# Program order for layer 2's scalings, and ScalarE for layer 3's transpose copies

## The chip, the cores and the metric

The kernel runs on one core of one Trainium2 chip. The metric is the device time of one execution, in microseconds (us). A core has five engines that run side by side and meet at semaphores: TensorE for matmuls and transposes (PE in the profile, PEld for its weight loads), VectorE (DVE), ScalarE (ACT), GpSimd (POOL) and SyncE (SP), which only issues transfers. Transfers are issued from the queues of SP, ACT and POOL.

## What is computed

The program is a chain of four residual layers on 8 images of 56 x 56 pixels with 192 channels. Each layer first normalises its input over 32 groups of channels, then adds what it computes to it:

```python
x = x + toeplitz_gated_unit(_gn(x))      # layer 0
x = x + window_attention(_gn(x))         # layer 1
x = x + L2(_gn(x))                       # layer 2
x = x + L3(_gn(x))                       # layer 3

def L2(x):
    proj = x @ W_in + b_in                       # 192 -> 384 channels
    local = depthwise_conv_3x3(proj)
    mixed = 0.25 * (lr + rl + tb + bt) + local   # decaying sums in four directions
    return layernorm(mixed) @ W_out + b_out

def L3(x):
    y = layernorm(depthwise_conv_7x7(x))
    return (gelu(y @ w0 + b0) @ w1 + b1) * gamma
```

The change touches the entry of layer 2 (its group normalisation, and the transfer of its first image) and the entry of layer 3 (the copies behind its transposes). All data is float32.

## The kernel before

The image is held with channels on the partitions, its upper half in partitions 0 to 63 and its lower half in 64 to 127, as three chunks of 64 channels. Stages follow one another, each a loop over the 8 images; between some of them the data goes through DRAM, since the convolutions run over all images with channels as the outer loop.

**Layer 2's projection** (about 3570 to 3860 us). `layer2_image` (line 787) makes a tile `x2` from a pool of two, clears its border rows on GpSimd and loads two halves on the queue that it is given. The loop at line 1313 starts the load of image b+1 on SP and then calls `layer2_in` for image b. That function (line 797) makes `xn`, the normalised image: three scalings on VectorE, one for each chunk (line 803), and two edge memsets on GpSimd (lines 806 and 807). Then come 15 groups of matmuls into four PSUM buffers (line 815), each followed by a bias add on VectorE (line 823) that writes the projected tile `pt`, and the store of `pt` to DRAM on SP. `xn` and `pt` have two buffers each. At line 1310 the first image is loaded on POOL's queue; the two lines after it load the weights on ACT's queue. After the sixth image, line 1318 finishes the last image's group statistics. Ahead of the stage, layer 1's last image is stored by rows: 54 stores on SP at line 612, of which 30 fall after 3553 us.

No order is written by hand in this stage. A scheduler places the instructions of each engine by its own estimate of when their inputs are ready; it may put an instruction of a later image ahead of one of an earlier image if it takes the former for ready sooner.

**The joint stage** (about 4521 to 5040 us) makes layer 2's output and layer 3's input together. It runs in 8 x 4 groups of rows: for each group three output channels chunks j are multiplied (`layer2_out`, line 960) and added to the image (line 965), while the next group is scaled (lines 936 on VectorE and 938 on ScalarE), transposed (line 947) and evacuated from PSUM on ScalarE (line 948). In the steps 3 to 8 of an image's twelve, VectorE also takes the layer norm statistics of the next image (line 190). Between these go the steps of the generator `layer3_in` (line 968) for the image before: its group statistics, three normalising scalings on GpSimd (line 985), and then, for each of three chunks, 15 transposes in four PSUM tiles (line 1006) with the copies into `zt` (lines 993 and 995), and a store of `zt` to DRAM. From two PSUM buffers the first and third tile are copied by VectorE, the second and fourth by ScalarE; the fourth has two extra single-row copies, one on each engine. VectorE's order in this stage is the program's own (`manual_schedule`), that of TensorE and ScalarE is the scheduler's. The last image's `layer3_in` runs alone at the end of the stage.

Of the kernel before, what the change touches and what calls it, by code (L numbers as in the profile page):

```python
# [52 lines left out]
PH = NPAIR // 2  # L53
# [24 lines left out]
def kernel(ctx: ExitStack, tc: tile.TileContext, a: dict, out: bass.AP):  # L78
    nc = tc.nc
# [61 lines left out]
    def gn_piece(st, x, t):  # L141

        for j in range(3):
            nc.vector.bn_stats(st[:, j, t], x[:, j, bass.ts(t, TT)])

    def gn_aggregate(st, mv):
        for j in range(3):
            nc.vector.bn_aggr(mv[:, j, :], st[:, j].rearrange("p t s -> p (t s)"))

    def gn_finish(mv, sc, sh, pool, psum, ptag):  # L150


        n = mv.shape[1]

        def over_groups(v, name):
            if ptag == "mm":
                ps = psum.tile([128, 512], F32, name=name, tag="mm", bufs=3)
            elif ptag == "y":
                ps = psum.tile([128, TT], F32, name=name, tag="y")
            elif ptag == "gn":  # L160
                ps = psum.tile([128, 3], F32, name=name, tag="gn", bufs=1)
            else:
                ps = psum.tile([128, 2, 512], F32, name=name, tag=ptag)[:, 0]
            ps = ps[:, 0:3 * n].rearrange("p (n j) -> p n j", j=3)
            for j in range(3):
                ks = [k for k in range(3) if abs(j - k) < 2]
                for k in ks:
                    nc.tensor.matmul(
                        ps[:, :, j], gmath[:, 2 * k + j, :], v[:, :, k], start=(k == ks[0]), stop=(k == ks[-1])
                    )  # L170
            return ps

        mean = pool.tile([128, n, 3], F32, name="gh_mean")
        nc.vector.tensor_copy(mean, over_groups(mv[:, :, :, 0], "gh_m"))
        d = pool.tile([128, n, 3], F32, name="gh_d")
        nc.vector.tensor_tensor(d, mv[:, :, :, 0], mean, ALU.subtract)
        nc.vector.tensor_tensor(d, d, d, ALU.mult)
        nc.vector.tensor_tensor(d, d, mv[:, :, :, 1], ALU.add)
        yield
        nc.scalar.activation(sc, over_groups(d, "gh_v"), AF.Sqrt, bias=eps5)  # L180
        nc.vector.reciprocal(sc, sc)
        nc.vector.scalar_tensor_tensor(sh, mean, -1.0, sc, ALU.mult, ALU.mult)

    def run(steps):
        for _ in steps:
            pass
# [152 lines left out]
    def layer0_load(b, pool):  # L339
        x = pool.tile([128, 3, NH], F32, name="x0")  # L340
        nc.gpsimd.dma_start(x, a["x"][b])
        return x
# [444 lines left out]
    def layer2_image(b, xpool, queue):  # L787

        x = xpool.tile([128, 3, R2, W], F32, name="x2")
        nc.gpsimd.memset(x[0:64, :, 0], 0.0)  # L790
        nc.gpsimd.memset(x[64:128, :, R2 - 3:R2], 0.0)
        src = x2[b].rearrange("(j p) (h w) -> p j h w", p=64, w=W)
        queue.dma_start(x[0:64, :, 1:R2], src[:, :, 0:R2 - 1])
        queue.dma_start(x[64:128, :, 0:R2 - 3], src[:, :, R2 - 1:H])
        return x

    def layer2_in(b, x, pool, psum, w_in, b_in):

        sc, sh = scsh2[:, b, 0], scsh2[:, b, 1]
        xn = pool.tile([128, 3, R2, 64], F32, name="xn2")  # L800
        nc.gpsimd.memset(xn[:, :, :, W:64], 0.0)
        for j in range(3):
            nc.vector.tensor_scalar(
                xn[:, j, :, 0:W], x[:, j], sc[:, j:j + 1], sh[:, j:j + 1], ALU.mult, ALU.add
            )
        nc.gpsimd.memset(xn[0:64, :, 0, 0:W], 0.0)
        nc.gpsimd.memset(xn[64:128, :, R2 - 3:R2, 0:W], 0.0)
        pt = pool.tile([128, C2, P2], F32, name="pt")
        nh = R2 // 2
        for i in range(nh):  # L810
            ns = 2 if i + nh < P2 else 1
            ps = psum.tile([128, 2, 512], F32, name="pin")
            for j in range(3):
                for s in range(ns):
                    nc.tensor.matmul(
                        ps[:, s, 0:C2], xn[64 * s:64 * s + 64, j, 2 * i:2 * i + 2].rearrange("p h w -> p (h w)"),
                        w_in[64 * s:64 * s + 64, j], start=(j == 0), stop=(j == 2),
                    )

            v = 0 if i == 0 else 2 if i + nh == P2 - 1 else 1  # L820
            dims = [list(z) for z in pt.ap]
            dst = bass.AP(pt.tensor, pt.offset + i, [dims[0], [nh, ns], [P2, C2]])
            nc.vector.tensor_tensor(dst, ps[:, 0:ns, 0:C2], b_in[:, v, 0:ns], ALU.add)

        n = CG2 if b + 1 == nimg else 0
        if n:
            nc.sync.dma_start(pd[b][:, 0:n], pt[:, 0:n])
        nc.sync.dma_start(pd[b][:, n:C2], pt[:, n:C2])
# [139 lines left out]
    def layer3_in(b, x, zp, pool, psum):  # L968

        sc = pool.tile([128, 1, 3], F32, name="sc3")  # L970
        sh = pool.tile([128, 1, 3], F32, name="sh3")
        st = pool.tile([128, 3, NTH, 6], F32, name="gh_st")
        mv = pool.tile([128, 1, 3, 2], F32, name="gh_mv")
        for t in range(NTH):
            gn_piece(st, x, t)
            if t % 2:
                yield
        gn_aggregate(st, mv[:, 0])
        finish = gn_finish(mv, sc, sh, pool, psum, "gn")
        next(finish)  # L980
        yield
        run(finish)

        for j in range(3):
            nc.gpsimd.tensor_scalar(
                zp[:, j, 1:H // 2 + 1, 0:W], x[:, j].rearrange("p (h w) -> p h w", w=W),
                sc[:, 0, j:j + 1], sh[:, 0, j:j + 1], ALU.mult, ALU.add,
            )
        yield

        def to(dst, src, eng):
            if eng:
                nc.scalar.copy(dst, src)
            else:
                nc.vector.tensor_copy(dst, src)

        for j in range(3):
            zt = pool.tile([OP, 64, NB], F32, name="zt")
            nc.gpsimd.memset(zt[:, :, 0:1], 0.0)
            nc.gpsimd.memset(zt[:, :, NB - 1:NB], 0.0)  # L1000
            for g, m0 in enumerate(range(0, PH + 1, 4)):
                yield
                tp = psum.tile([OP, 4, 2, 64], F32, name="zps")
                nm = min(4, PH + 1 - m0)
                for i in range(nm):
                    nc.tensor.transpose(  # L1006
                        tp[:, i].rearrange("p s c -> p (s c)"),
                        zp[:, j, 2 * (m0 + i):2 * (m0 + i) + 2].rearrange("p h w -> p (h w)"), ident,
                    )

                n2 = min(nm, PH - m0)
                dst = zt[:, :, 1 + m0:1 + m0 + n2]
                dst = bass.AP(dst.tensor, dst.offset, [list(dst.ap[0]), [1, n2], [PH, 2], [NB, 64]])
                to(dst, tp[:, 0:n2], g % 2)
                if nm > n2:

                    to(zt[:, :, 1 + 2 * PH], tp[:, n2, 1], 0)
                    to(zt[0:64, :, 1 + PH], tp[0:64, n2, 0], 1)
            nc.sync.dma_start(zd[b][:, 64 * j:64 * j + 64], zt)

    def convolve(first, dwb):
# [50 lines left out]
    def layer3_image(b, pool):  # L1072
        x = pool.tile([128, 3, NH], F32, name="x3")
        nc.sync.dma_start(x, xd[b])
        return x
# [100 lines left out]
    with ExitStack() as st:  # L1176
# [6 lines left out]
        x = layer0_load(0, pool)  # L1183
# [8 lines left out]
        for b in range(nimg):  # L1192
# [12 lines left out]
            if b + 1 < nimg:  # L1205
                x = layer0_load(b + 1, pool)
# [5 lines left out]
    with ExitStack() as st:  # L1212
# [8 lines left out]
        images, x = ExitStack(), []  # L1221
# [13 lines left out]
    with ExitStack() as st:  # L1235
# [20 lines left out]
        xpool = x.pop(0)  # L1256
# [49 lines left out]
    with ExitStack() as st:  # L1306
        xpool = st.enter_context(tc.tile_pool(reuse_waits="tile", name="l2x", bufs=2, side="right"))
        pool = st.enter_context(tc.tile_pool(reuse_waits="tile", name="l2i", bufs=2))
        psum = st.enter_context(tc.tile_pool(reuse_waits="tile", name="l2ip", bufs=4, space=PSUM))
        x = [layer2_image(0, xpool, nc.gpsimd)]  # L1310
        w_in = resident("w_in", nc.scalar, pool)
        b_in = resident("b_in", nc.scalar, pool)
        for b in range(nimg):
            if b + 1 < nimg:
                x.append(layer2_image(b + 1, xpool, nc.sync))
            layer2_in(b, x[b], pool, psum, w_in, b_in)
            if b == nimg - 3:
                run(gn_finish(mv2[:, last], scsh2[:, last, 0], scsh2[:, last, 1], pool, psum, "pin"))
    with ExitStack() as st:
# [8 lines left out]
        x = [load_halves(pool, x2[0], "x2o")]  # L1328
# [54 lines left out]
    with ExitStack() as st:  # L1383
# [9 lines left out]
        x = [layer3_image(0, pool)]  # L1393
# [122 lines left out]
```

## Time and profile before

| what | us |
|---|---|
| median of 3 runs (6226.7 to 6247.08) | 6227.99 |
| the profiled execution | 6250.54 |
| its span, first to last instruction | 6248.8 |
| TensorE, busy | 5549.3 (89%) |
| VectorE, busy | 3450.3 (55%) |
| ScalarE, busy | 2251.5 (36%) |
| GpSimd, busy | 1328.0 (21%) |
| line 803, scalings (24) | 26.1 busy, 1145 ns each |
| line 815, matmuls (1392) | 237.7 busy, 47.6 idle ahead |
| line 823, bias adds of 768 elements (112) | 169.9 busy, 1542 ns each |
| line 995, copies of 512 (48) and of 64 elements (24) on VectorE | 51.7 and 6.6 busy, 1077 and 276 ns each |
| line 993, copies of 512, 256 and 64 elements (24 each) on ScalarE | 26.1, 15.0 and 6.5 busy, 1089, 627 and 269 ns each |

Busy time is the time in which an engine has an instruction of its own running. Idle time ahead is the time an engine stood still before the instructions of a group; it counts only where that engine sets the pace. In the lines of the profile an arrow in square brackets names what ended the wait.

### The profile page before, as it was taken

Reading aid. Unit: us, or ns where it says so; the run is one execution under the profiler, and the core shown is the slowest. Engines: PE = TensorE matmul, PEld = TensorE weight load, DVE = VectorE, ACT = ScalarE, POOL = GpSimd, SP = SyncE. Lnnn points to the kernel's source line nnn. Section 1 sums busy time; section 2 is a strip of 40 time slices with the busy share of each in tenths; the row PEclk is TensorE's granted clock in tenths of the full one; section 3 lists DMA queues with packets and bytes.
Section 4 is the critical chain, followed back from the end, with each engine's and each line's share of the span. In section 5 each row is a group of like instructions: output and inputs, shape, how many; then the busy total and the mean of one; then the engine's idle time right before and its main releaser. Section 6 shows DMA issues by size and latency. Waiting matters only on the chain. (4 is left out here: it accounts for less than half of the span.)

```text
span 6248.8 us, 126609 instructions
## 1 busy us (share of the span) xinstructions
PE 5549.3 (89%) x55636; PEld 3585.7 (57%) x55636; DVE 3450.3 (55%) x4800; ACT 2251.5 (36%) x2932; POOL 1328.0 (21%) x869
## 2 busy tenths in 40 slices
PE   6799989999999888888888688999888889799999
PEld 5577766666666454445444466767544479544444
DVE  5677766556565344444444376888788710433331
ACT  2334444344444233333333200445455510233333
POOL 1100025444444122121212101333300100110100
PEclk8899989999999888878888798999999989899999
DMA  6799986666665515545442586677667579421210
GB/s 165 186 216 214 191 242 255 264 261 258 256 256 213 80 34 60 60 60 56 56 48 41 67 239 226 209 232 239 189 167 208 162 288 331 154 82 64 72 57 24
DMA packets 1034540, 1013.11 MB, mean 162 GB/s; under 512 B 826136, under 2 KB 958196, under 8 KB 1007220
## 3 DMA queue, kind: packets, MB, share of 16 engines
q1 hardware_dynamic: 1019424, 940.93, 54.0%
q0 software_dynamic: 8832, 41.81, 2.2%
q10 hardware_dynamic: 5732, 22.27, 1.1%
q8 instruction: 437, 7.16, 0.5%
q14 instruction: 115, 0.94, 0.0%
HBM read 676.28 MB, written 345.08 MB: 163 GB/s over the span
## 5 line engine op out<-in xcount | busy, mean ns | idle before, releaser
L371 PE MATMUL qv<-w_qv_sb,xn 64*112 64x288 f32 x5376 | 722.1, 425 | 50.3 <-DVE act L377 46.9
L409 POOL COPY lc<-lt 128x896 f32<-128x896 f32 (+1 forms) x320 | 572.1, 1805 | 624.5 <-PE op L417 608.4
L371 PEld LDWEIGHTS qv<-w_qv_sb,xn 64*112 64x112 f32 x5376 | 535.0, 184 | 232.5 <-DVE act L377 63.2
L378 ACT ACTIVATE act<-act 112x576 f32<-112x576 f32 x448 | 299.9, 682 | 462.8 <-DVE act L377 425.8
L1145 PE MATMUL ph<-y,w_sb 64*128 64x392 f32 x2304 | 398.4, 498 | 6.5 <-ACT hid L1149 6.5
L429 PE MATMUL pj<-xn,w_p_sb 64*128 64x392 f32 (+1 forms) x1920 | 374.0, 516 | 14.0 <-issue 10.7
L1156 PE MATMUL po<-hid,w_sb 128*64 128x392 f32 x2304 | 386.3, 494 | 0.0
L417 PEld LDWEIGHTS op<-rc,lc 128*56 128x56 f32 x9216 | 310.6, 137 | 127.2 <-issue 61.8
L417 PE MATMUL op<-rc,lc 128*56 128x56 f32 x9216 | 342.1, 222 | 45.2 <-POOL lc L409 26.1
L450 PE MATMUL y<-pp,w_o_sb 128*64 128x392 f32 (+1 forms) x1920 | 357.3, 505 | 18.9 <-DVE x L458 10.2
L377 DVE TENSOR_TENSOR act<-qv,b_qv 112x576 f32<-112x576 f32 x448 | 320.7, 751 | 85.4 <-PE qv L371 85.0
L1163 DVE TENSOR_TENSOR x<-x,z 128x392 f32<-128x392 f32 x96 | 70.4, 733 | 522.8 <-ACT z L1161 522.8
L409 ACT COPY rc<-rt 128x896 f32<-128x896 f32 (+1 forms) x160 | 256.9, 1606 | 240.6 <-PE op L417 226.7
L727 POOL TENSOR_TENSOR e<-e,mx 128x1176 f32<-128x1176 f32 x64 | 139.9, 2185 | 954.3 <-DVE mx L726 899.4
L866 PE MATMUL cv<-zc,wt 128*128 128x224 f32 x1536 | 313.7, 356 | 24.1 <-DMA zc<-pd 24.1
L866 PEld LDWEIGHTS cv<-zc,wt 128*128 128x128 f32 x1536 | 290.9, 190 | 67.8 <-issue 51.6
L443 DVE TENSOR_TENSOR pp<-pp,ot 128x784 f32<-128x784 f32 (+1 forms) x160 | 154.6, 966 | 306.6 <-ACT pp L434 288.3
L677 PE MATMUL qk_ps<-xr,wg 64*96 64x392 f32 x1536 | 309.7, 512 | 15.1 <-ACT qk L683 13.5
L1145 PEld LDWEIGHTS ph<-y,w_sb 64*128 64x128 f32 x2304 | 220.4, 189 | 176.4 <-issue 26.0
L1046 PE MATMUL cps<-zc,wt 128*128 128x224 f32 x1536 | 299.5, 356 | 18.0 <-DMA zc<-zd 17.6
L1046 PEld LDWEIGHTS cps<-zc,wt 128*128 128x128 f32 x1536 | 289.5, 189 | 27.8 <-issue 20.4
L1156 PEld LDWEIGHTS po<-hid,w_sb 128*64 128x64 f32 x2304 | 162.6, 137 | 213.8 <-issue 213.8
(211 smaller groups left out, 9423.0 us busy)
## 6 DMA issues: line engine op xcount, KB each, us to landing
lt<-left SPq DMA_DIRECT2D x72, 1792.0 KB
rt<-right SPq DMA_DIRECT2D x72, 1792.0 KB
left<-qv SPq DMA_DIRECT2D x224, 252.0 KB
right<-qv SPq DMA_DIRECT2D x448, 126.0 KB
wt<-in_band_dram SPq DMA_DIRECT2D x23, 2048.0 KB
wt<-in_band_dram SPq DMA_DIRECT2D x11, 4096.0 KB
zc<-pd SPq DMA_DIRECT2D x187, 232.0 KB
pd<-pt SPq DMA_DIRECT2D x7, 5568.0 KB
```

Source lines behind the costliest of these rows:

```text
L371: nc.tensor.matmul(ps[s][:, which, 0:D1 // 2], xn[64 * s:64 * s + 64, j, bass.ts(i, 2 * W)], w_qv[64 * s:64 * s + 64, j, which, ns], start ...
L377: nc.vector.tensor_tensor(act, ps[s][:, :, 0:D1 // 2], b_qv[:, :, ns], ALU.add)
L378: nc.scalar.activation(act, act, AF.Silu)
L409: copy(c[:, 0:nu], raw.rearrange("p (w u d) -> p u d w", u=nu, d=64 // nu)[:, :, d0:d0 + 8])
L417: nc.tensor.matmul(op[64 * u:64 * u + W, i, :], lc[:, u, i], rc[:, u, i], start=True, stop=True)
L429: nc.tensor.matmul(ps[0:M, s, 0:TT], w_p[64 * s:64 * s + 64, j, d0:d0 + M], xn[64 * s:64 * s + 64, j, ts], start=(j == 0), stop=(j == 2),)
L450: nc.tensor.matmul(y[64 * s:64 * s + 64], w_o[0:M, c, 64 * j:64 * j + 64], pp[0:M, s], start=(c == gated[0][0]), stop=(c == gated[-1][0]),)
L677: nc.tensor.matmul(ps[s], wg[64 * s:64 * s + 64, j, c0:c0 + HC], xw[64 * s:64 * s + 64, j, gs], start=(j == 0), stop=(j == 2),)
L866: nc.tensor.matmul(dst, wt[:, c4 + i, 128 * q:128 * q + 128], zc[:, :, c4 + i, q:q + NPAIR], start=(q == 0), stop=(q == 1),)
L1046: nc.tensor.matmul(dst.rearrange("p (b n) -> p b n", n=NPAIR), wt[:, c4 + i, q * OP:(q + 1) * OP], zc[:, :, c4 + i, q:q + NPAIR], start=(q ...
L1145: nc.tensor.matmul(ps[:, s, 0:TT], w0[64 * s:64 * s + 64, j, m * 128:(m + 1) * 128], y[64 * s:64 * s + 64, j, ts], start=(j == 0), stop=(j ...
L1156: nc.tensor.matmul(ps[64 * s:64 * s + 64], w1[:, m, 64 * j:64 * j + 64], hid[:, m, s], start=(m == 0), stop=(m == 5),)
```

## The change

Three edits. The scalings of `layer2_in` are wrapped in `tc.keep_in_program_order`, which pins an instruction behind the one that was written before it on the same engine (an order alone, not a wait for its end). The copies behind layer 3's transposes all go to ScalarE. The first image of layer 2 is loaded on ACT's queue.

```diff
@@ layer2_in
         for j in range(3):
-            nc.vector.tensor_scalar(
+            tc.keep_in_program_order(nc.vector.tensor_scalar(
                 xn[:, j, :, 0:W], x[:, j], sc[:, j:j + 1], sh[:, j:j + 1], ALU.mult, ALU.add
-            )
+            ))
@@ layer3_in
-        def to(dst, src, eng):
-            if eng:
-                nc.scalar.copy(dst, src)
-            else:
-                nc.vector.tensor_copy(dst, src)
-
         for j in range(3):
...
-            for g, m0 in enumerate(range(0, PH + 1, 4)):
+            for m0 in range(0, PH + 1, 4):
...
-                to(dst, tp[:, 0:n2], g % 2)
+                nc.scalar.copy(dst, tp[:, 0:n2])
                 if nm > n2:
-                    to(zt[:, :, 1 + 2 * PH], tp[:, n2, 1], 0)
-                    to(zt[0:64, :, 1 + PH], tp[0:64, n2, 0], 1)
+                    nc.scalar.copy(zt[:, :, 1 + 2 * PH], tp[:, n2, 1])
+                    nc.scalar.copy(zt[0:64, :, 1 + PH], tp[0:64, n2, 0])
@@ layer 2's projection
-        x = [layer2_image(0, xpool, nc.gpsimd)]
+        x = [layer2_image(0, xpool, nc.scalar)]
         w_in = resident("w_in", nc.scalar, pool)
         b_in = resident("b_in", nc.scalar, pool)
```

In the program that the scheduler makes of it, VectorE's order in the projection is: the three scalings of an image, its 15 bias adds, the three scalings of the next image, and so on. On ACT's queue the first image's two loads stand behind both weight loads.

## The prediction, made before the changed kernel ran

> **What bounds the kernel now.** The chain of waits at the foot of the page is of little use: its shares add up to 22%, and asked for the stretch from 4460 us on it begins at 4937.03. So I went by stages. The line groups gave the start of each stage, a table of windows gave the busy time in it, and the timeline gave what happens at its edges. The columns of the windows are the stretch and its length, then busy time (count) of PE, PEld, DVE, ACT and POOL, the granted clock, the DMA share and GB/s.
>
> ```profile
> 3569.00:3616.00 47.00, 0.33 (x2) 0.33 (x4) 6.66 (x8) 1.28 (x1) 2.25 (x4) 0.53 0.73 140
> 3616.00:3860.00 244.00, 242.04 (x1420) 169.85 (x1418) 196.42 (x145) 0.26 (x1) 15.53 (x35) 0.97 0.68 223
> 4521.00:5040.00 519.00, 431.19 (x2395) 229.02 (x2393) 397.81 (x737) 274.03 (x389) 52.98 (x72) 0.92 0.62 180
> ```
>
> Row one is the gap ahead of layer 2's projection: 47 us with no engine at work. Row two is that projection: TensorE is busy 242.04 of 244 us, so nothing but TensorE sets its length. Row three is the joint stage (layer 2's output and layer 3's input): no engine is full over the whole of it.
>
> The timeline shows what ended the gap, and how an image follows the last:
>
> ```profile
> 3595.48 0.59 SPq L793 DMA_DIRECT2D x<-x  x1
> 3610.03 6.48 DVE L803 TENSOR_SCALAR xn<-x,scsh 128x1680 f32<-128x1680 f32 x6 [40.30 <-DMA x<-x]
> 3615.67 176.30 PE L815 MATMUL pin<-w_in_sb,xn 64*128 64x384 f32 x1044 [47.62 <-POOL xn L806]
> 3646.88 0.85 DVE L823 TENSOR_TENSOR pt<-pin,b_in_sb 128x384 f32<-128x384 f32 x1 [0.39 <-PE pin L815]
> 3647.57 3.26 DVE L803 TENSOR_SCALAR xn<-x,scsh 128x1680 f32<-128x1680 f32 x3
> 3650.89 0.23 POOL L806 MEMSET xn<- 64x168 f32 x1 [3.22 <-DVE xn L803]
> ```
>
> Six scalings stand together at 3610.03: those of images 0 and 1. In the built program image 1's first piece is ahead of image 0's three, so image 0 (loads issued at 3563.31 and 3563.97, landed 17.7 us after the second) waits for image 1, loaded at 3595.48. In exchange VectorE is one image ahead: the scalings at 3647.57 are image 2's, and TensorE runs 176.30 us without a break.
>
> For the joint stage, three windows inside one image's period, and the edge between the first two:
>
> ```profile
> 4861.00:4888.00 27.00, 19.69 (x121) 10.21 (x120) 26.79 (x45) 9.76 (x18) 0.33 (x2) 0.96 0.52 127
> 4888.00:4900.00 12.00, 10.23 (x48) 7.30 (x47) 6.56 (x12) 10.70 (x14) 0.33 (x2) 0.66 0.98 258
> 4900.00:4923.00 23.00, 22.81 (x131) 11.51 (x132) 16.14 (x37) 14.25 (x19) 1.42 (x1) 1.00 0.81 269
> ...
> 4886.33 1.17 DVE L995 COPY zt<-zps 128x512 f32<-128x512 f32 x2
> ...
> 4887.53 1.94 PE L1006 MATMUL zps<-ident,zp 128*128 128x128 f32 x8 [4.66 <-DVE zt L995]
> ```
>
> VectorE fills the first (26.79 of 27), ScalarE nearly the second (10.70 of 12), TensorE the third (22.81 of 23). The waits view says the same of the stage: layer 3's transposes wait for VectorE's copies 45.1 us (matmul) and 17.6 us (weight load), for ScalarE's 10.1 and 15.6.
>
> [...]after its 4.66 us gap the 5 us from 4887.5 have clock 0.50, and the 3.4 us behind the like gaps that end at 4698.0 and 4759.6 have 0.52 and 0.51. [...]from 3568 to 3580 the queues of POOL, ACT and SP have shares of 76.3, 22.6 and 4.7%, together one. [...]
>
> **Part 1, the scalings keep program order.** In the built program of the changed kernel each image's three scalings stand behind the last bias add of the image before. The look-ahead is gone at all seven edges between images. At each, TensorE now waits for: the last bias add (3646.88 to the next instruction, 0.69), three scalings (3.26), the step to GpSimd (0.06), its edge memset (0.23), the step back (about 0.05): 4.3 us. It waited for nothing there before. The gap is of the size that halves the clock: 3.4 to 5 us at half speed cost 1.7 to 2.5, I take 1.9. At the edge from image 5 to 6 the group statistics already stop TensorE (3791.9 to 3797.6, half clock to 3803.8), so only the 4.3 is added. Sum: 6 x (4.3 + 1.9) + 4.3 = 41.5 us. Nothing hides it, since TensorE is the bound of the stage. Bounds: 30 (no clock loss) to 50. Behind the waiting scalings stand only the next image's bias adds, which need them anyway; behind the stores on SP stand loads that have an image's time (some 33 us) to land. No cost there.
>
> **Part 2, image 0's load on ACT's queue.** It leaves POOL, where it was issued at 3563.31, and in the built order stands behind both weight loads on ACT; its two halves wait besides for one each of the last row stores of layer 1's image 7. In the old run the 30 stores left SP between 3553.68 and 3594; from 3568 to 3580 they got 4.7% because POOL's load took 76.3%. Without it they can end up to 12 us sooner, near 3583. Then image 0's and image 1's loads (2352 KB, or 2.41 MB, each) run beside one another: 4.82 MB at the 207 GB/s of 3600 to 3608 is 23.3 us, plus 2.9 to start (image 1's took 14.55 = 11.6 + 2.9): both land near 3608, image 0 some 2 to 3 us sooner, say 3605. Three scalings and a memset later TensorE starts, at 3608.6 in place of 3615.67: 7 us gained. Bounds: 16 gained (image 0 gets the engines alone) to 8 lost (the stores end as late as before).
>
> Layer 2's projection in sum: 41.5 - 7 = +34.5, between +20 and +50.
>
> **Part 3, copies in the joint stage.** VectorE loses 72 copies (51.7 + 6.6 us), ScalarE gains as many of the same length. They count where VectorE is the bound: in the window of 27 us it makes copies of 1.14, 1.23, 1.10 and 1.17 us, 4.64 in sum; 22.4 us of other work stay, above TensorE's 19.69. So the statistics, the next image's scalings and its first transposes come 4 to 4.6 us sooner[...]. Given back: in the new order ScalarE takes the copies in pairs, those of the third piece later, among layer 2's evacuations where TensorE is full; a pair (2.2 us) ahead of an evacuation holds the next transposes up by about 1 us. I take 3.7 net in each of 6 images. In the last image's period VectorE has no statistics ahead (13.67 busy of 29 between 4981 and 5010): nothing. In the tail after 5026.96 both engines copied in turn in 12.0 us; ScalarE alone needs 9 x 1.09 + 3 x 0.63 + 6 x 0.27 = 13.3 and its steps: +1.7. Sum: -22.2 + 1.7 = -20.5, between -42 and 0.
>
> **Sum.** 34.5 - 20.5 = +14. Against the profiled execution's own 6250.54 us that is 6264.5. That execution is 0.36% above the median of the runs shown, so I put the change on the median: 6228 + 14 = 6242 us. A measurement of this kernel can tell 0.3%, or 18.7 us, from no change.
>
> **Rivals.**
> - *Forecast* (0.52): both effects as above, from -8 to +32; slower by over 0.3% in 0.22 of it, within in 0.30.
> - *Not slower: the joint stage gives back more* (0.21). Place: the edge at 4887.53. If the copies (4.64), the rest of the gap and its half clock (2.5) all go, 7 us an image are saved: 6 x 7 - 1.7 = 40, and the sum is -6, or 6222 us. It decides from (34.5 + 1.7)/6 = 6.0 us an image; past 9.1, or with small clock losses, it is faster by over 0.3%. For it: 62.7 us of waits on VectorE's copies. Against: ScalarE is full in the next window. Faster 0.12, within 0.09.
> - *ScalarE becomes the joint stage's bound* (0.20): with the copies moved it has 338 of 519 us in all, and 10.70 of 12 in one window already. Nothing is gained there, the tail costs 1.7: +36, 6264 us. Slower.
> - *Image 0 arrives late* (0.07): the row stores take as long as before, and the loads share: part 2 turns to +8, sum +29, 6257 us. Slower 0.05, within 0.02.
>
> Sums: faster 0.12, within 0.3% 0.41, slower 0.47. The range takes the rivals in and leaves out a tenth at each end: 6212 to 6272.
>
> **What would show it.** Right: seven TensorE gaps of some 4.3 us ahead of the projection's matmuls, ended by GpSimd's memset, each with a dip in the clock; 275 to 290 us from the first to the last of these matmuls in place of 243; the first of them near 3608; no transposes of layer 3 waiting for VectorE; the period of an image in the joint stage near 58 us where it was 61.7. Wrong: no gaps, or scalings that run while matmuls do; a start before 3600 or after 3616; a joint stage shorter by over 40 us, or no shorter at all.

## The result, and the profile after

The changed kernel takes 6237.23 us, the median of 12 runs (6212.07 to 6248.5), and the kernel before, run beside it, 6229.72 us, also of 12 (6216.59 to 6249.95). The two medians are 7.5 us apart; over all runs the ratio is 1.0005, or +3 us, with a 95% interval from 0.9992 to 1.0019, in time between 5 us less and 12 us more. That is no difference that this measurement can tell. Behind it stand three effects of 17 to 44 us that cancel.

The profiled execution of the changed kernel has a span of 6230.6 us, 18.2 less than that of before. This says nothing of the change: layers 0 and 1, whose code is the same, ended 18.9 us sooner in it (last matmul of layer 1 at 3549.20 in place of 3568.05 us). So stages are compared here by their own lengths, and the start of the projection is counted from that last matmul. Line numbers of the changed kernel differ: the scalings are line 804, the upper edge memset 807, the projection's matmuls 816, layer 3's transposes 1001 and their copies 1009.

The windows view of the changed kernel, cut at the edges of its own stages (columns as in the prediction):

```profile
3549.20:3579.78 30.58, 0.00 (x0) 0.00 (x1) 5.14 (x8) 1.28 (x1) 2.63 (x3) 0.56 0.74 156
3579.78:3867.28 287.50, 256.36 (x1420) 148.91 (x1420) 201.22 (x146) 0.26 (x1) 14.39 (x33) 0.92 0.61 196
4522.59:5019.54 496.95, 434.55 (x2394) 224.00 (x2393) 350.33 (x665) 315.39 (x458) 53.14 (x72) 0.92 0.64 187
```

| stage | before | after | difference |
|---|---|---|---|
| last matmul of layer 1 to first of the projection | 47.62 | 30.58 | -17.0 |
| projection, first to last matmul | 243.31 | 287.50 | +44.2 |
| joint stage, first output matmul to last transpose of layer 3 | 516.50 | 496.95 | -19.5 |
| sum | | | +7.6 |

The timeline of the changed kernel at the start of the projection and at the edge from image 1 to image 2:

```profile
3561.26 0.69 ACTq L793 DMA_DIRECT2D x<-x  x1
3561.99 0.72 ACTq L794 DMA_DIRECT2D x<-x  x1
3575.87 3.57 DVE L804 TENSOR_SCALAR xn<-x,scsh 128x1680 f32<-128x1680 f32 x3 [24.99 <-DMA x<-x]
3576.10 1.09 POOL L790 MEMSET x<- 64x168 f32 x1 [31.63 <-DMA x<-x]
3576.11 0.59 SPq L793 DMA_DIRECT2D x<-x  x1
3579.78 31.27 PE L816 MATMUL pin<-w_in_sb,xn 64*128 64x384 f32 x174 [30.58 <-POOL xn L807]
...
3647.65 0.84 DVE L824 TENSOR_TENSOR pt<-pin,b_in_sb 128x384 f32<-128x384 f32 x1 [0.39 <-PE pin L816]
3648.33 3.25 DVE L804 TENSOR_SCALAR xn<-x,scsh 128x1680 f32<-128x1680 f32 x3
3651.64 0.23 POOL L807 MEMSET xn<- 64x168 f32 x1 [3.21 <-DVE xn L804]
3651.93 30.98 PE L816 MATMUL pin<-w_in_sb,xn 64*128 64x384 f32 x174 [4.32 <-POOL xn L807]
```

In its first part, image 0 waits for nothing but its own load and starts alone; the load of image 1 leaves SP at 3576.11, when that of image 0 has just landed. In the second, a bias add, three scalings and a memset stand one behind the other, and TensorE waits 4.32 us for them. Each of the seven edges looks like this, and an image that took 29.3 us from its first matmul to its last in the kernel before takes 31.0 to 32.3 us behind its gap.

For the joint stage, two groups of the kernel before and the same two of the changed kernel (busy time and mean, then the idle time ahead and what ended it):

```profile
L1006 PE MATMUL zps<-ident,zp 128*128 128x128 f32 x360 | 61.2, 308 | 57.9 <-DVE zt L995 45.1 <-ACT zt L993 10.1 <-POOL zp L985 2.6
L947 PE MATMUL tp<-ident,yt 112*128 112x112 f32 x672 | 104.0, 289 | 39.7 <-DVE yt L936 34.3 <-ACT y L948 5.3
...
L1001 PE MATMUL zps<-ident,zp 128*128 128x128 f32 x360 | 56.8, 299 | 6.5 <-ACT zt L1009 3.5 <-POOL zp L986 2.6
L948 PE MATMUL tp<-ident,yt 112*128 112x112 f32 x672 | 106.6, 290 | 66.1 <-DVE yt L937 57.7 <-ACT y L949 7.9
```

Layer 3's transposes no longer wait for VectorE (before: 45.1 us), and for ScalarE's copies only 3.5 us. In place of that, layer 2's own transposes (the second row of each pair) wait longer for VectorE's scaled rows, 57.7 us where they waited 34.3: VectorE still sets the pace at the edge inside an image, with less to do.

### The profile page after: what moved, and what is told of

It is laid out like the page before. It is cut to its first block, busy times and chain, and to the rows that moved or that the text cites. A ratio compares the mean times of both kernels' runs of the same rounds, so it can differ in the third digit from the quotient of the medians.

```text
span 6230.6 us, 126592 instructions
## 1 busy us (share of the span) xinstructions
PE 5550.5 (89%) x55636; PEld 3552.3 (57%) x55636; DVE 3403.1 (55%) x4728; ACT 2293.7 (37%) x3004; POOL 1320.7 (21%) x867
## 5 line engine op out<-in xcount | busy, mean ns | idle before, releaser
L429 PE MATMUL pj<-xn,w_p_sb 64*128 64x392 f32 (+1 forms) x1920 | 375.2, 517 | 14.5 <-issue 10.8
L816 PE MATMUL pin<-w_in_sb,xn 64*128 64x384 f32 x1392 | 253.0, 514 | 60.8 <-POOL xn L807 60.8
```

The lines of the kernel that those rows point to most:

```text
L429: nc.tensor.matmul(ps[0:M, s, 0:TT], w_p[64 * s:64 * s + 64, j, d0:d0 + M], xn[64 * s:64 * s + 64, j, ts], start=(j == 0), stop=(j == 2),)
```

## The experiments

All ratios are against the kernel before, run beside each on the same chip, with 95% intervals; the kernel before had medians of 6216 and 6215 us there, so one thousandth is 6.2 us. The stages in the traces are compared with the one trace of the kernel before. Two of the kernels below leave layer 2's start as it was (the copies alone, and VectorE's time put back): there TensorE starts 44.33 and 44.35 us behind layer 1's last matmul, and the projection takes 241.69 and 243.21 us, in place of 47.62 and 243.31. So a start is known to some 3 us, and each gain at the start that is given below may be about 3 us too large.

### The program order alone

```diff
+            tc.keep_in_program_order(nc.vector.tensor_scalar(
```

(on all scalings; the first image stays on GpSimd's queue, the copies as before)

> The kernel before with the program order alone. In the changed kernel TensorE began the projection 30.6 us after its last matmul of layer 1 (before: 47.6), and the projection then took 287.5 us (before: 243.3). Theory: the order does both. It costs the seven edges (+44), and it frees image 0 from waiting for image 1; image 0 still comes on GpSimd's queue here, where it landed 13.6 us after the last matmul, so TensorE should begin some 18 us after it, 30 us sooner than before: sum +14, near 6244, ratio 1.0022. Rival: the sooner start came from the other queue, which lets the row stores through. Then the start stays near 47 us, sum +44, near 6273, ratio 1.007.

Measured: ratio 1.0041 (1.0028 to 1.0054), or +25 us. In the trace the projection takes 287.98 us, and it starts 25.33 us behind layer 1's last matmul. The timeline of this kernel shows what the start waited for:

```profile
3540.95 3.28 DVE L803 TENSOR_SCALAR xn<-x,scsh 128x1680 f32<-128x1680 f32 x3 [10.47 <-DMA x<-x]
3553.00 0.59 SPq L793 DMA_DIRECT2D x<-x  x1
3553.00 0.23 POOL L790 MEMSET x<- 64x168 f32 x1 [27.66 <-DMA x<-x]
3553.27 0.52 POOL L791 MEMSET x<- 64x504 f32 x1
3553.84 0.23 POOL L806 MEMSET xn<- 64x168 f32 x1
3554.13 2.29 PE L815 MATMUL pin<-w_in_sb,xn 64*128 64x384 f32 x6 [25.33 <-POOL xn L806]
```

The scalings of image 0 end at 3544.25, 15.4 us behind that last matmul, as the theory had it. But the edge memset that TensorE needs stands on GpSimd behind two memsets for image 1's tile, and these wait for layer 1's row stores until 3553.00. So the order costs +44.7 and gains 22.3, not 30. The rival, that only the other queue made the sooner start, falls: without that queue the start is 5.3 us sooner still than in the changed kernel.

### The first image's queue alone

```diff
-        x = [layer2_image(0, xpool, nc.gpsimd)]
+        x = [layer2_image(0, xpool, nc.scalar)]
```

> The kernel before with only image 0's load on ScalarE's queue. In this build VectorE scales image 0, then image 1, then takes image 0's bias adds. Theory: image 0 can start 17 us sooner, as in the changed kernel, but the bias adds stand behind image 1, which lands some 42 us after the last matmul of layer 1: TensorE fills its four PSUM buffers (8 to 10 us) and stops for about 7 us, with a half clock behind it. Net -5 to -9, near 6223; no gaps at the other edges. Rival: the queue alone brings the whole 17 us, near 6213. If image 0 and image 1 share the engines: no gain, 6229.

Measured: ratio 0.9981 (0.9973 to 0.9989), or -12 us. The interval, -17 to -7, reaches from the theory's -5 to -9 to the rival's -17 (6213), so the time alone does not decide; the timeline of this kernel does:

```profile
3567.80 10.41 PE L815 MATMUL pin<-w_in_sb,xn 64*128 64x384 f32 x48 [29.71 <-POOL xn L806]
...
3578.73 3.29 DVE L803 TENSOR_SCALAR xn<-x,scsh 128x1680 f32<-128x1680 f32 x3 [11.27 <-DMA x<-x]
3581.93 8.69 DVE L823 TENSOR_TENSOR pt<-pin,b_in_sb 128x768 f32<-128x768 f32 x6
...
3583.50 6.82 PE L815 MATMUL pin<-w_in_sb,xn 64*128 64x384 f32 x32 [5.28 <-DVE pt L823]
```

TensorE starts 17.9 us sooner than before, fills its PSUM buffers and then waits 5.28 us, since image 0's bias adds stand behind image 1's scalings (3578.73), which wait for their load. The projection takes 249.29 us in place of 243.31. So -17.9 + 6.0 = -11.9: the theory's mechanism, and not the whole of the sooner start.

### The copies alone

```diff
-                to(dst, tp[:, 0:n2], g % 2)
+                to(dst, tp[:, 0:n2], 1)
...
-                    to(zt[:, :, 1 + 2 * PH], tp[:, n2, 1], 0)
+                    to(zt[:, :, 1 + 2 * PH], tp[:, n2, 1], 1)
```

> The kernel before with only the copies on ScalarE. Theory: the joint stage loses 19 to 22 us, as it did in the changed kernel (516.5 to 497.0 us from its first output matmul to its last transpose); an image's period is 58 us; the gap at the edge inside an image falls from 4.6 to 2.9 us and the clock no longer halves after it; near 6209, ratio 0.9968. Rival: one period of before, of 67.2 us, was an accident of that execution, so that the gain is 14 to 15 us, near 6215; or part of it comes from the other edits, and the gain is under 10.

Measured: ratio 0.9963 (0.9952 to 0.9973), or -23 us. The joint stage takes 498.44 us, 18 less than before, and the periods of its images are 56.5 to 62.0 us. Both rivals fall: the kernels with the old copies (program order alone, queue alone) have joint stages of 518.05 and 518.35 us, and each has one period of 65 to 67 us too, at another image. The gap at the edge is 2.9 us, as expected; what was expected of the clock is wrong (behind one of these gaps it is 0.50 from 4783.70 to 4785.40), as the section on the prediction shows for the changed kernel.

### VectorE's time put back

```diff
                 to(dst, tp[:, 0:n2], 1)
+                if g % 2 == 0:
+                    nc.vector.tensor_tensor(idle, idle, idle, ALU.add)
                 if nm > n2:
+                    nc.vector.tensor_tensor(idle[:, 0:190], idle[:, 0:190], idle[:, 0:190], ALU.add)
```

(on top of the copies alone)

> All copies on ScalarE as in the changed joint stage (nothing else of the change), and on VectorE, in the places of the 72 copies that left, additions on a tile of its own that nothing reads and nothing waits for (912 elements, some 1.08 us, and 190 elements, some 0.28 us). This kernel does more work than the reference asks for. Theory: the stage is held by VectorE's time in the first part of an image's period, so the gain of 19 us goes again: joint stage 513 to 518 us, same as before, ratio 1.000. Rival: what held it was that TensorE waited for VectorE to free the two PSUM buffers; then the gain stays, joint stage 497 to 501 us, ratio 0.9965.

Measured: ratio 0.9998 (0.9985 to 1.0011), joint stage 515.77 us. The whole gain is gone, although no instruction outside VectorE waits for these additions (48 of 1.10 us and 24 of 0.36 us, medians). In the timeline of this kernel, at the edge inside an image:

```profile
4836.07 3.98 DVE L190 BATCH_NORM_STATS2 ln_st<-ml 112x6 f32<-112x384 f32 x5
4841.10 1.10 DVE L1016 TENSOR_TENSOR idle<-idle 128x912 f32<-128x912 f32 x1
4842.23 0.36 DVE L1018 TENSOR_TENSOR idle<-idle 128x190 f32<-128x190 f32 x1
4843.09 1.18 DVE L936 TENSOR_SCALAR yt<-ml,ln_rs,ln_mr 112x384 f32<-112x384 f32 x2
4843.77 1.29 PE L947 MATMUL tp<-ident,yt 112*128 112x112 f32 x4 [5.64 <-DVE yt L936]
```

TensorE stands 5.64 us until VectorE, behind its statistics and the additions, has scaled the next rows. Where it waited for VectorE to free PSUM before, it waits for VectorE's next product here. VectorE's time alone, then, can hold the stage, and the rival that the gain stays falls. That the length comes out like that of before is in part luck: of the 17.3 us over the copies alone, 10.1 are idle time of TensorE (75.8 us in place of 65.7, where before had 85.5), and 7.2 are time in which it is busy at a lower mean clock (0.89 in place of 0.92). That the old copies held the stage through VectorE's time alone, and in no part through the PSUM buffers, is therefore not shown.

### The order for two images only, with the copies

```diff
+            if b < 2:
+                tc.keep_in_program_order(scaling)
```

> The kernel before with the copies on ScalarE and the program order for images 0 and 1 alone: after image 0's bias adds VectorE scales images 1 and 2 together and is one image ahead from there on. Image 0 comes on GpSimd's queue. Theory: start -30, one edge +6.3, joint stage -20: sum -44, near 6186, ratio 0.993. Rival, if the sooner start came from the other queue: -14, near 6216.

Measured: ratio 0.9947 (0.9930 to 0.9963), or -33 us. The start is 26.12 us behind the last matmul (-21.5, held by the same memsets on GpSimd), the projection takes 249.37 us (+6.1, one edge) and the joint stage 496.65 us (-19.9): the sum is -35. The expected -44 missed the memsets; the rival's -14 lies outside the interval (-44 to -23).

### The edge cleared chunk by chunk

```diff
             tc.keep_in_program_order(nc.vector.tensor_scalar(
                 xn[:, j, :, 0:W], x[:, j], sc[:, j:j + 1], sh[:, j:j + 1], ALU.mult, ALU.add
             ))
-        nc.gpsimd.memset(xn[0:64, :, 0, 0:W], 0.0)
+            tc.keep_in_program_order(nc.gpsimd.memset(xn[0:64, j, 0, 0:W], 0.0))
```

(on top of the changed kernel)

> The changed kernel with the upper edge of xn cleared chunk by chunk, each right behind its scaling, so that an image's first matmuls wait for one scaling and not for three. The idle time at an image's edge is cut up: about 2.2 us, two matmuls, 0.9 us, two matmuls, 0.9 us. In the changed kernel an edge cost 6.3 us: a gap of 4.3 us and some 2 us of half clock. Theory: the half clock comes from the length of the unbroken gap, so it goes; an edge costs about 3.5 us, seven edges give back 20 us: 287.5 to about 268 us for the projection, ratio to before 0.997. Rival: the clock follows the idle share over a while, so it halves all the same; then only the overlap of some 0.9 us at an edge is saved, 281 us, ratio 0.9995.

Measured: ratio 0.9981 (0.9971 to 0.9991), or -12 us, against +3 for the changed kernel. The projection takes 267.70 us: the expected 268, but not for the expected reason. From the windows view of this kernel (the clock is the third column from the end), the first 3.4 us behind two of the edges:

```profile
3591.38:3594.80 3.42, 3.08 (x16) 1.46 (x18) 2.15 (x3) 0.00 (x0) 1.43 (x5) 1.00 0.98 417
...
3623.66:3627.06 3.40, 3.40 (x12) 1.67 (x14) 1.92 (x2) 0.00 (x0) 1.41 (x5) 0.56 0.98 419
```

Both gaps were of 2.10 us. The first is followed by full clock, the second by half; of the seven gaps of this size five are followed by half clock. What tells them apart is the grid of 3.413 us on which the clock changes in this trace (its 11 changes from 3562.65 to 3798.17 us lie whole multiples of 3.413 us apart, to within 0.02). These are the two steps of the grid in which the two gaps end:

```profile
3589.97:3593.38 3.41, 1.83 (x8) 0.60 (x8) 3.34 (x4) 0.00 (x0) 0.43 (x4) 1.00 0.98 418
...
3620.69:3624.10 3.41, 1.31 (x7) 0.49 (x5) 3.04 (x4) 0.00 (x0) 0.84 (x2) 1.00 0.49 209
```

The first gap began in the step ahead: TensorE is idle for 0.7 us in that one and for 1.6 us in this one, and the clock stays. The second lies whole in one step, idle for 2.1 us, and the next step runs at half clock. The other gap behind which the clock stays, the one that ends at 3690.41, is split in the same way (0.6 and 1.6 us). TensorE's idle time in the projection fell from 31.1 to 16.6 us (before: 0.9); of the 24.4 us that the edges still cost, 15.7 are idle time and 8.7 the clock. More was won by overlap than the theory had, and less by the clock.

### An order written by hand

```diff
-            nc.vector.tensor_tensor(dst, ps[:, 0:ns, 0:C2], b_in[:, v, 0:ns], ALU.add)
+            tc.keep_in_program_order(nc.vector.tensor_tensor(dst, ps[:, 0:ns, 0:C2], b_in[:, v, 0:ns], ALU.add))
+            if i == 11:
+                scale_next()
...
-        nc.gpsimd.memset(xn[0:64, :, 0, 0:W], 0.0)
+        tc.keep_in_program_order(nc.vector.memset(xn[0:64, :, 0, 0:W], 0.0))
```

(`scale_next` makes the next image's `xn`, its three scalings pinned; image 0 is scaled ahead of the loop)

> The kernel before with image 0 on GpSimd's queue, VectorE's order in the projection written by hand (each image's scalings behind the twelfth bias add of the image before), the upper edge of xn cleared on VectorE and not on GpSimd, and the copies on ScalarE, in turn with VectorE for the last image. Where TensorE began 25 to 26 us after its last matmul of layer 1 with image 0 on GpSimd's queue, the scalings were done at 15.5, and GpSimd stood in a clearing of image 1's tile, which waits for the row stores, ahead of the edge of xn. Theory: without that, the start is at 16 to 18 us (-30), no edge gap, so 243 us for the projection, joint stage -20, tail -1.5: sum -51, ratio 0.992. Rival: image 0's bias adds wait for b_in or for image 1 (landed 39 to 42 us after the last matmul), and half of the sooner start is lost in the first image: -36, ratio 0.994.

Measured: ratio 0.9932 (0.9915 to 0.9949), or -42 us: faster than both kernels. The timeline of this kernel:

```profile
3554.70 3.29 DVE L803 TENSOR_SCALAR xn<-x,scsh 128x1680 f32<-128x1680 f32 x3 [11.22 <-DMA x<-x]
3558.08 0.20 DVE L806 MEMSET xn<- 64x168 f32 x1
...
3558.54 176.39 PE L819 MATMUL pin<-w_in_sb,xn 64*128 64x384 f32 x1044 [16.73 <-DVE xn L806]
```

The first matmul comes 16.73 us behind layer 1's last, in place of 47.62, and six images run without a break, as in the kernel before. The start is 30.9 us sooner, the projection takes 243.86 us (+0.6) and the joint stage 498.87 us (-17.6): -48 in the traces, within the measured interval (-53 to -32). The rival of -36 is inside that interval too, but its mechanism is not in the trace: nothing stops image 0. The last image's copies, in turn on both engines again, did not show the expected 1.5 us: the end of the stage from its last output matmul took 30.47 us here, and 28.1 to 30.5 in all the other kernels, whichever engine copied.

## Why the prediction was right, and where not

The forecast was +14 us, with a range from 6212 to 6272 us that holds no difference too; it gave slower by over 0.3% a chance of 0.47, and a change within 0.3% one of 0.41. Measured were +3 us (-5 to +12), and +7.6 in the two traces: within the range, and below the +14. Its two large effects, the edges and the copies, have their signs and nearly their sizes; the start was missed by 10 us. Term by term:

**Part 1, the edges: right, +41.5 against +44.2.** The gap is 4.32 us at each edge, where the sum of bias add, scalings and memset gave 4.3, and half clock goes with each of them, as with the nine gaps of 3.80 to 4.83 us in the joint stage of before. The rest is the clock: idle time grew by 30.2 us and the projection by 44.2, so the clock cost 14.0, where 6 x 1.9 = 11.4 was taken. The windows of the changed kernel behind two edges show how:

```profile
3615.37:3618.77 3.40, 3.40 (x12) 1.90 (x14) 0.00 (x0) 0.00 (x0) 1.25 (x3) 0.50 0.99 419
3618.77:3622.17 3.40, 3.40 (x16) 1.92 (x14) 1.53 (x1) 0.00 (x0) 0.00 (x0) 0.62 0.97 411
...
3651.93:3655.33 3.40, 3.40 (x12) 1.91 (x14) 0.00 (x0) 0.00 (x0) 1.25 (x3) 0.52 0.99 419
3655.33:3658.73 3.40, 3.40 (x24) 2.08 (x22) 2.46 (x2) 0.00 (x0) 0.00 (x0) 0.98 0.97 419
```

Behind the first edge the clock stays low for most of a second window, behind the next it does not; images of 32.2 and 31.0 us take turns. In this trace the stretches of full and of half clock last whole multiples of 3.413 us: half clock lasts 6.83 us at the first of these two edges (3614.52 to 3621.35) and 3.41 us at the next (3652.07 to 3655.48), although both gaps are of 4.32 us. So what a gap cost here went with where it fell between two such steps: the clock took about 1.7 and 2.9 us of an image by turns, where the prediction had one price of 1.9. At the edge from image 5 to 6 it took nothing new, as forecast (32.1 us before, 32.3 after).

**Part 2, image 0's load: the direction right, the size not, -7 against -17.0 (-14 against the two other kernels with the old start).** The failed step is "Then image 0's and image 1's loads (2352 KB, or 2.41 MB, each) run beside one another". They did not. The row stores left SP sooner, as said (the last 13.9 us behind layer 1's last matmul; the prediction's 3583 is 15 behind it). But image 1's tile has to wait for all of these stores, and the last two, issued at 3561.82 and 3562.47, landed only at 3575.09 and 3575.92: they took over 13 us beside image 0's load, issued from 3561.26 on. In the kernel with the program order alone no large load was under way when the last row stores left: the last one, issued at 3550.93, had landed by 3553.00, when the load that waits for it was issued. So image 0 had the DMA engines nearly alone and landed at 3575.74, 14.5 us after its issue, where image 1 had taken 14.55 alone in the old trace. That is the case of the bound of 16 gained ("image 0 gets the engines alone"), which the prediction kept in its range and didn't take. By its own list of signs, a start before 3600 us was to count against it: in the old execution's time the start is at 3598.6. A second thing was not seen at all: the gain does not need the queue. It comes when image 0's scalings no longer stand behind image 1's, and the order alone does that: the start is at 25.33 us, and with the queue added at 30.58. In the build with the queue alone image 0's scalings stand first too; it gains 17.9 us at the start and gives 6.0 back in the first image.

**Part 3, the copies: the size right, -20.5 against -19.5, one reason wrong.** The first six periods of an image, each from the first normalising scaling on GpSimd to that of the next image, sum to 372.2 us before and 350.3 after: 3.65 an image, where 3.7 was taken. The additions in the place of the copies show that VectorE's time can cost the stage as much. What fails is the gap: with the next image's first transposes 4 to 4.6 us sooner, that of 4.66 us would nearly close. It fell to 2.91 us and is still followed by half clock (0.50 from 4874.04 to 4877.45). The gain is idle time: TensorE idled 85.5 us in the stage before and 62.4 after, 23.1 less, more than the stage gained. The clock gave nothing (0.92 in the stage before and after), so it is in part luck that the size came out. What was given back is where the prediction put it: between 4600 and 5020 us the weight loads of layer 2's transposes wait 43.0 us for ScalarE's evacuations, where they waited 33.3. The tail of +1.7 measured +1.5 in these two traces, but lies within what the tail varies by itself (28.1 to 30.5 us over all kernels).

**The rivals.** ScalarE did not become the bound; it is busy for 315.39 us of the stage, where the prediction's 338 does not follow from its own numbers (274.03 + 51.7 + 6.6 = 332.3). The joint stage did not give 6 us an image. Image 0 did not come late, although the row stores that were to delay it did land late, for image 1. One reading was loose: in the gap of 47 us it was TensorE that had no work; VectorE was busy for 6.66 us of it.

## What to carry to other kernels

When a scheduler's order is replaced by the program's, ask for every stage what it had moved ahead, and why: here one order held back the first image (22.3 us with the program's order alone, 30.9 with the edge's memset moved as well) and hid 6 us at each of seven edges, and writing that one look-ahead by hand kept the second without the first. To find whether an engine's time counts in a stage that no engine fills, add work on it that nobody waits for, and see whether the stage grows (here by 17.3 us for some 61 us of additions); then read in the trace whether it grew by idle time or by the clock. And follow an instruction's neighbours on its own engine: a memset of 0.2 us on GpSimd held TensorE for over 9 us because of what stood in front of it.

## What the runs showed of the hardware

- Half clock went with TensorE's gaps of 3.80 to 4.83 us in the joint stage of before in nine of nine cases, with the gaps of 2.3 to 2.9 us at every image of the changed joint stage (seven, each with 0.50 behind it), and with the gaps of 2.06 to 2.10 us at the edges cleared chunk by chunk in five of seven cases. Where in the clock's grid of 3.413 us such a short gap lay went with it: the two that were split over two steps, 0.6 or 0.7 and 1.6 us, left the clock full, and the other five lay in one step to within 0.1 us. A single step at half clock costs 1.7 us and two in a row 3.4, an estimate from their lengths of 3.41 and 6.83 us at 0.50.
- The clock also fell with no gap of 1 us in the 15 us ahead: in the joint stage of before it was low from 4848.3 to 4858.5 while TensorE worked. It cost about 5 us: in the one period of 67 us TensorE is busy for 57.9 us, in the one ahead for 52.0. Its place changed from kernel to kernel: with the additions on VectorE it fell like that three times, at about 4805.1, 4866.5 and 4928.0, and in the changed joint stage not at all. In the step of the grid just ahead (4844.88 to 4848.30) TensorE was busy for 1.88 us with the group statistics' matmuls of a single column (line 168), and idle for 0.19 us. The clock stays full behind a step with 1.88 and 0.10 us (4783.45 in the kernel before), and behind three with 1.72 and 0.19 us in the changed kernel. No run took these matmuls away, and the cause is not shown.
- Two row stores of 2.2 KB took 13.3 and 13.5 us to land beside one load of 2.41 MB issued at the same time. Who shares the DMA engines with a large load may be what the next load waits for.
